# Order of the phases in one period of a two-layer graph attention kernel: score products, mask multiplications and GpSimd's sums on a Trainium2 core

## Chip, core and metric

The kernel runs on one core of a Trainium2 chip. The metric is the device time of one launch in microseconds (us), lower is better. Engines are named as the profile names them: PE is TensorE (matmuls, with PEld for its weight loads), DVE is VectorE, ACT is ScalarE, POOL is GpSimd, SP is SyncE (which issues nearly all DMAs).

## What is computed

64 graphs of 256 nodes with 512 features pass through two attention layers. Layer 0 has 8 heads of 64 features, layer 1 has 4; everything is float32. Shortened:

```python
h = relu(layernorm(x))                      # layer 0
m = h @ map_w.T + map_b
n = m_heads / norm(m_heads)
cos = n @ n.T ; cos_adj = (cos * ~adj) > 0.1
q, k = m @ q_w.T, m @ k_w.T
p = softmax(where(adj, -1e10, q k.T / 8)) * keep
A = cos_adj * p
x = x + relu((A @ (h @ gcn_map_w.T)) @ gcn_W.T / (A.sum(-1) + 1))
h = relu(layernorm(x))                      # layer 1
q, k, v = h @ Wq, h @ Wk, h @ Wv
attn = softmax(where(adj, q k.T / 8, -max))
x = x + (attn @ v) @ Wo + bo
```

## The kernel before

All instructions of all engines are issued in an order written out by hand (`manual_schedule`): each engine executes its own instructions in the order in which the code emits them, and semaphores between engines are put in where one instruction needs another's result or its buffer. The unit of the order is `period(i)` (line 556). A period works on up to four graphs at once: layer 0's attention of graph `g` (number i), layer 1's attention of graph `b` (i-1), the projections of layer 0 for `nx` (i+1), and the normalised, transposed input of `n2` (i+2). There are 65 periods, of which most have all four.

Projections are done by a seven-product scheme on halves (`seven_products`, line 260). It is a generator: each `next(...)` emits one portion. For the map (`m`), messages (`s`), queries (`q`), keys (`k`) and layer 1's queries and keys (`j`), the order of the `next` calls decides the order of the matmuls. A product group's result tile "z" (`pz`, line 311) is used several times in a row: the next portion writes it as soon as DVE has read the previous contents with `out(...)` (line 301).

Attention of a graph goes by head pairs: `NKC` = 4 pairs for layer 0, `NIC` = 2 for layer 1. For each pair c:
- `products` (line 395) forms transposed scores. Each matmul contracts over 64 rows only, so two heads run side by side in two halves of the array. Such matmuls read "64*128" in the profile, the projections "128*128".
- `exps` (line 404) takes the exponentials on ACT, from two PSUM banks into the SBUF tile `e` (128 x 1024 in all).
- `masked` (line 411) multiplies by the mask on DVE: one instruction of 128 x 1024 (line 417 for layer 0, line 415 for layer 1).
- `halves` (line 419) adds the two halves of `e` along the nodes on POOL into `d` (line 421): the first part of the softmax's denominator.
- Layer 0 only: `units` (line 382) multiplies the map by reciprocal lengths on DVE (one instruction of 128 x 1024, line 384), `cosines` (line 431) forms the cosine products from it, again with 64 rows, and `far_off` (line 442) thresholds them: ACT makes a small tile `up`, and DVE overwrites `e` in four instructions (line 451). `far_added` and `far_back` (lines 456 and 460) correct `d` on POOL by what was left (lines 458 and 465), and `far_back` finishes `e` on DVE (line 463). As `far_off` overwrites `e`, it has to come after `halves` of the same pair has read it.

`halved` (line 351) calls `left_factors` (line 250): four POOL instructions on the finished map `mT` (lines 254 to 257, tile `sm`). `shifts` (line 220) is a short DVE chain for `n2`: a reciprocal (line 201) and an instruction of 128 x 2 (line 224) that reads two SBUF operands.

PSUM is one ring of eight banks: each new tile takes the bank of the tile eight allocations earlier and waits until that one has been read.

Of the kernel before, what the change touches and what calls it, by code (L numbers as in the profile page):

```python
# [147 lines left out]
def fast_path(ctx, tc, a, w, chk, out):  # L148
# [8 lines left out]
    H0, NKC = D // DH, D // P  # L157
    INNER = a["Wq"].shape[1]
    H1, NIC = INNER // DH, INNER // P
# [81 lines left out]
    def join(g, k):  # L241
        nc.scalar.copy(g.bits[:, k], g.turn[:, k])
# [108 lines left out]
    def halved(g):  # L351
        g.left_m = left_factors(g.mT, "sm", g.i)
# [29 lines left out]
    def units(g):  # L382

        nc.vector.tensor_mul(g.nT, g.nT, g.mT)
# [10 lines left out]
    def products(rows, cols, c, name):  # L395

        ps = [bank(f"{name}_{s}", [P, NT, S]) for s in range(2)]
        for j in range(NT):
            for s in range(2):
                h = slice(s * DH, (s + 1) * DH)  # L400
                nc.tensor.matmul(ps[s][:, j, :], rows[h, c, j * P:(j + 1) * P], cols[h, c, :], start=True, stop=True)  # L401
        return ps

    def exps(ps, name):

        e = sb2.tile([P, 2, NT * S], F32, tag="e", name=f"e{name}", bufs=6)
        for s, p in enumerate(ps):
            nc.scalar.activation(e[:, s, :], p.rearrange("p j q -> p (j q)"), AF.Exp, scale=SCALE)  # L408
        return e

    def masked(e, mask, edges):

        m = mask.rearrange("p j q -> p (j q)")[:, None, :].to_broadcast([P, 2, NT * S])
        if edges:
            nc.vector.scalar_tensor_tensor(e, m, 0.5, e, op0=ALU.is_lt, op1=ALU.mult)  # L415
        else:
            nc.vector.tensor_mul(e, e, m)  # L417

    def halves(e, name):
        d = sb2.tile([P, 2, S], F32, tag="d", name=f"d{name}", bufs=6)  # L420
        nc.gpsimd.tensor_add(d, e[:, :, :S], e[:, :, S:])  # L421
        return d
# [133 lines left out]
    def period(i):  # L556
        g = graphs.get(i) if i < B else None
        b, nx, n2 = graphs.get(i - 1), graphs.get(i + 1), graphs.get(i + 2)
        def off_edges(cs):
            for c in cs if g else ():  # L560
                masked(g.e[c], g.mask, edges=False)
                g.d[c] = halves(g.e[c], f"0_{i}_{c}")


        if b:
            b.e1 = [exps(products(b.k1T, b.q1T, c, f"sc1_{b.i}_{c}"), f"1_{b.i}_{c}") for c in range(NIC)]
            for c in range(NIC):
                masked(b.e1[c], b.mask, edges=True)
            if b.last:
                for t in range(NT):  # L570
                    values_in(b, t)
            else:
                b.d1 = [halves(b.e1[c], f"1_{b.i}_{c}") for c in range(NIC)]
        if nx:
            m, s = mapped(nx), messages(nx)
            next(m)
        if g:
            for c in range(NKC):
                g.e[c] = exps(products(g.kT, g.qT, c, f"sc0_{i}_{c}"), f"0_{i}_{c}")
        if nx:  # L580
            next(s)
        off_edges((0, 1))
        if nx:
            next(m)
        off_edges((2,))
        if nx:
            next(m)
            next(s)
            next(m)
            halved(nx)  # L590

        if g:
            for c in range(NKC):
                far_off(g, c, cosines(g, c))
                if c == 0:
                    off_edges((3,))
            for c in range(NKC):
                far_added(g, c)
        if n2:
            shifts(n2, f"0_{n2.i}")  # L600
        if nx:
            q = queries(nx)
            next(q)
            next(s)
        if n2:
            sent(n2, f"0_{n2.i}", 0)
        if nx:
            next(q)
            squares(nx)
            next(s)  # L610
        if n2:
            sent(n2, f"0_{n2.i}", 1)
        for c in range(NKC):
            if g:
                far_back(g, c)
            if nx and c < 3:
                next((q, s, q)[c])
        if nx:
            lengths(nx, norms(nx))

        if i == 0:
            w.finish_seven(w.wqk1)
        if b:
            sums1(b)
            values1(b)
        if g:
            g.avs = sb1.tile([P, NKC, S], F32, tag="wide", name=f"avs{i}")
            g.sms = sb1.tile([P, S], F32, tag="sms", name=f"sms{i}")
            values(g, 0)
            values(g, 1)  # L630
            sums(g)
        if n2:
            joined(n2, f"0_{n2.i}")
            join(n2, 0)
        if nx:
            k = keys(nx)
            next(k)
        if b:
            nc.scalar.activation(b.rz, b.rz, AF.Copy, accum_out=chk[:, b.i, 3:4])
        if g:  # L640
            sums_back(g)
            heads_back(g)
        if n2:
            join(n2, 1)
        if nx:
            next(k)
        if n2:
            edges(n2)
        if b:
            divided(b)  # L650
        if g:
            moments(g, f"1_{i}")
        if nx:
            next(k)
        if g:
            deviations(g)
        if g:
            normalized(g, f"1_{i}")
        if nx:
            nc.scalar.activation(nx.rn, nx.rn, AF.Sqrt)  # L660

        nc.scalar.activation(spare[:, 1:], spare[:, :1], AF.Exp)
        if b:
            for t in range(NT):
                result(b, t)
                if b.last:
                    nc.sync.dma_start(out=out_t[b.i][:, t], in_=b.xs[:, t])
            if not b.last:
                nc.sync.dma_start(out=out_t[b.i], in_=b.xs)
        if i + 3 < B:  # L670
            graphs[i + 3] = load(i + 3)
        if g:
            g.h1T = turned(g, f"1_{i}", "wide")
            j = queries_keys1(g)
            for t in range(NT):
                nc.gpsimd.tensor_add(g.xs[:, t, :], g.xs[:, t, :], w.bo_b)
        if nx:
            next(k)
        if g:
            next(j)  # L680
        if nx:
            nc.vector.reciprocal(nx.rn, nx.rn)
            spread(nx)
        if g:
            next(j)
        if g:
            next(j)
            if not g.last:
                values_in(g, 0)
            next(j)  # L690
        if n2:
            n2.left_h = left_factors(n2.hT, "sh", n2.i)
        if i + 3 < B:
            moments(graphs[i + 3], f"0_{i + 3}")
        if g and not g.last:
            values_in(g, 1)
        if nx:
            units(nx)

    def normal_input(g):  # L700
        g.hT = turned(g, f"0_{g.i}", "hT")
# [2 lines left out]
    with tc.manual_schedule():  # L704
        spare = small.tile([P, 2], F32, tag="spare", name="spare", bufs=1)
        nc.vector.memset(spare, 0.0)
        graphs = {0: load(0)}
        w.load_map()
        gws = [sb2.tile([P, 2, D], F32, tag="e", name=f"gw{k}", bufs=6) for k in range(2)]
        w.load_folded(gws)  # L710
        w.load_scores()
        graphs.update({n: load(n) for n in range(1, min(3, B))})
        w.load_rest()

        def normal(n):
            moments(graphs[n], f"0_{n}")
            deviations(graphs[n])
            normalized(graphs[n], f"0_{n}")

        g = graphs[0]  # L720
        normal(0)
        normal_input(g)
        edges(g)
        w.finish_seven(w.wm)
        m = mapped(g)
        next(m)
        next(m)
        w.fold(gws, bank, w.put_seven)
        next(m)
        w.finish_seven(w.wq)  # L730
        next(m)
        halved(g)
        squares(g)
        w.finish_seven(w.wk)
        q, k, s = queries(g), keys(g), messages(g)
        next(q)
        lengths(g, norms(g))
        w.fold_bias(sb2.tile([P, NKC, P], F32, tag="xn", name="gbb"), bank)
        w.finish_seven(w.wc)
        for step in (k, q, k, q, k, q, k):  # L740
            next(step)
        nc.scalar.activation(g.rn, g.rn, AF.Sqrt)
        nc.vector.reciprocal(g.rn, g.rn)
        spread(g)
        if B > 1:
            edges(graphs[1])
            normal(1)
        nc.scalar.activation(spare[:, 1:], spare[:, :1], AF.Exp)
        for _ in range(5):
            next(s)  # L750
        units(g)
        if B > 1:
            normal_input(graphs[1])
        if B > 2:
            moments(graphs[2], "0_2")
        for i in range(B + 1):
            period(i)
# [298 lines left out]
```

## Time and profile before

| | |
|---|---|
| median of 3 runs | 3695.11 us (3693.84 to 3696.11) |
| span of the profiled execution | 3695.8 us, TensorE clock granted 0.996 |
| PE busy | 3651.0 us (99%) |
| PE weight loads | 3091.7 us (84%) |
| DVE busy | 2774.1 us (75%) |
| ACT busy | 1904.1 us (52%) |
| POOL busy | 2348.0 us (64%) |

The steady periods are equal: the score products of successive graphs start 56.58 us apart. A timeline lists the instructions of an engine in order of time, successive ones of the same kind merged: start (us from the span's start), duration, engine, line, operation, output <- inputs, shapes, count, and in brackets the idle time before it and what ended it. All times named below are of the period whose first score product starts at 1813.46 us; later periods repeat it 56.58 us further on. In fp32 each matmul and weight load of the code is two records.

### The profile page before, as it was taken

The page shows a single profiled execution, that of the slowest core. Times are in us where ns is not written, and L with a number is a line of the kernel's source. Part 1 is how long each engine was busy: PE and PEld are TensorE (multiplying, and loading weights), DVE is VectorE, ACT ScalarE, POOL GpSimd, SP SyncE. Part 2 cuts the span into 40 slices and gives each one's busy share as a digit, 9 for nine tenths or more (in the row PEclk, how much of TensorE's full clock was granted, in tenths as well). Part 3 has the DMA queues.
Part 4 walks back from the last instruction along what each step waited for, and adds up shares of the span by engine and source line. Part 5 has one row for each costly group of instructions (what it writes and reads, how often), then busy time and mean ns, then how long its engine had stood idle before and what let it go on. Part 6 is the DMA issues. An engine that isn't in the chain of part 4 may idle for free.

```text
span 3695.8 us, 76415 instructions
## 1 busy us (share of the span) xinstructions
PE 3651.0 (99%) x29153; PEld 3091.7 (84%) x29153; DVE 2774.1 (75%) x5288; ACT 1904.1 (52%) x4480; POOL 2348.0 (64%) x2044
## 2 busy tenths in 40 slices
PE   7999999999999999999999999999999999999997
PEld 7888888888888888888888888888888888888885
DVE  6777777777777777777877777777777777777775
ACT  3555555555555555555555555555555555555543
POOL 3667566666665665666766666666666667566663
PEclk9999999999999999999999999999999999999998
DMA  3111211211211112112112121121121112211211
GB/s 109 46 50 50 57 44 54 60 42 53 56 47 54 45 53 59 43 53 59 43 54 51 50 57 44 53 60 43 52 56 46 54 47 52 58 43 53 60 29 35
DMA packets 361008, 191.71 MB, mean 52 GB/s; under 512 B 272449, under 2 KB 326977, under 8 KB 360641
## 3 DMA queue, kind: packets, MB, share of 16 engines
q1 hardware_dynamic: 358368, 186.76, 19.0%
q8 instruction: 232, 3.80, 0.4%
q14 instruction: 136, 1.11, 0.1%
q10 hardware_dynamic: 2272, 0.04, 0.0%
HBM read 94.67 MB, written 34.34 MB: 35 GB/s over the span
## 4 chain that ended last, share of the span: by engine, by line
PE 96%; DVE 1%; DMA 1%; POOL 0%; issue 0%; ACT 0%; SPq 0%; DVEq 0%; ACTq 0%; POOLq 0%
PE sc L401 9%; PE av L428 9%; PE p_k L276 6%; PE p_q L276 6%; PE p_m L276 6%; PE p_qk L276 6%; PE p_s L271 6%; PE p_o L553 6%; PE p_v L520 6%; PE p_q_z L276 5%; PE co L438 5%; PE p_qk_z L276 5%; PE p_k_z L276 5%; PE p_m_z L276 5%; PE p_s_z L271 4%; PE sm L481 2%
## 5 line engine op out<-in xcount | busy, mean ns | idle before, releaser
L421 POOL TENSOR_TENSOR d<-e 128x512 f32<-128x512 f32 x382 | 716.2, 1900 | 199.5 <-DVE e L415 191.6
L408 ACT ACTIVATE e<-sc 128x512 f32<-128x512 f32 x768 | 389.9, 620 | 382.1 <-PE sc L401 375.6
L417 DVE TENSOR_TENSOR e<-e,mask 128x1024 f32<-128x1024 f32 x256 | 465.0, 1836 | 55.0 <-ACT e L408 55.0
L506 POOL TENSOR_TENSOR xs<-xs,o 128x512 f32<-128x512 f32 x128 | 188.5, 1494 | 385.5 <-DVE o L504 385.5
L465 POOL TENSOR_TENSOR d<-d,e 128x512 f32<-128x512 f32 x252 | 321.3, 1275 | 170.9 <-DVE e L463 169.2
L254 POOL TENSOR_TENSOR sh<-hT 128x256 f32<-128x256 f32 x128 | 93.6, 731 | 495.1 <-ACT hT L217 317.8
L458 POOL TENSOR_TENSOR d<-d,e 128x512 f32<-128x512 f32 x252 | 312.2, 1268 | 0.0
L451 DVE SCALAR_TENSOR_TENSOR e<-co,e 128x256 f32<-128x256 f32 (+1 forms) x1024 | 282.0, 343 | 35.8 <-ACT up L448 34.7
L448 ACT ACTIVATE up<-co,below 128x128 bf16<-128x128 f32 x512 | 159.6, 366 | 183.2 <-PE co L438 177.4
L553 PE MATMUL p_o<-wo,own 128*128 128x512 f32 x512 | 234.0, 600 | 9.8 <-DVE own L548 9.8
L520 PE MATMUL p_v<-wv,hT 128*128 128x256 f32 x1024 | 242.2, 379 | 0.0
L401 PE MATMUL sc<-qT,kT 64*128 64x256 f32 x2048 | 238.3, 382 | 0.0
L428 PE MATMUL av<-e,sem 128*64 128x256 f32 x2048 | 232.7, 380 | 0.0
L463 DVE SCALAR_TENSOR_TENSOR e<-far,e 128x256 f32<-128x256 bf16 x256 | 230.9, 903 | 0.0
L401 PEld LDWEIGHTS sc<-qT,kT 64*128 64x128 f32 x2048 | 192.9, 187 | 27.5
L428 PEld LDWEIGHTS av<-e,sem 128*64 128x64 f32 x2048 | 147.1, 137 | 75.2 <-DVE e L463 1.1
L491 DVE RECIPROCAL r<-rt 128x16 f32<-128x16 f32 x64 | 16.5, 258 | 253.3 <-PE rt L489 253.3
L520 PEld LDWEIGHTS p_v<-wv,hT 128*128 128x128 f32 x1024 | 184.9, 190 | 20.2 <-issue 0.3
L194 DVE BATCH_NORM_STATS2 st<-xs 128x6 f32<-128x512 f32 x256 | 173.8, 679 | 25.1 <-POOL xs L506 22.1
L438 PE MATMUL co<-nT 64*128 64x256 f32 (+1 forms) x2048 | 184.9, 330 | 0.0
L553 PEld LDWEIGHTS p_o<-wo,own 128*128 128x128 f32 x512 | 93.6, 193 | 104.7 <-issue 101.7
L231 ACT ACTIVATE xn<-xs,shift,rs 128x512 f32<-128x512 f32 x124 | 100.5, 810 | 156.1 <-POOL d L458 153.6
(198 smaller groups left out, 9350.0 us busy)
## 6 DMA issues: line engine op xcount, KB each, us to landing
xs<-in_x_dram SPq DMA_DIRECT2D x64, 512.0 KB
nT<-by_rn SPq DMA_DIRECT2D x128, 256.0 KB
out_dram<-xs SPq DMA_DIRECT2D x63, 512.0 KB
own<-by_rz SPq DMA_DIRECT2D x128, 128.0 KB
ad<-in_adj_dram SPq DMA_DIRECT2D x64, 64.0 KB
far<-up SPq DMA_TRANSPOSE x256
turn<-flat SPq DMA_TRANSPOSE x248
mask<-adb SPq DMA_TRANSPOSE x128
```

The lines of the kernel that those rows point to most:

```text
L271: nc.tensor.matmul(region, src[:, c, :], wt[:, block, c, :], start=p not in opened, stop=True, skip_group_check=True)
L276: nc.tensor.matmul(region[:, f, :], wt[:, block, c, f * P:(f + 1) * P], src[:, c, :], start=p not in opened, stop=True, skip_group_check=True)
L401: nc.tensor.matmul(ps[s][:, j, :], rows[h, c, j * P:(j + 1) * P], cols[h, c, :], start=True, stop=True)
L408: nc.scalar.activation(e[:, s, :], p.rearrange("p j q -> p (j q)"), AF.Exp, scale=SCALE)
L417: nc.vector.tensor_mul(e, e, m)
L421: nc.gpsimd.tensor_add(d, e[:, :, :S], e[:, :, S:])
L428: nc.tensor.matmul(av[s * DH:(s + 1) * DH, n, :], vs[:, j, (h0 + s) * DH:(h0 + s + 1) * DH], q[:, s, j * S:(j + 1) * S], start=(j == 0), s ...
L438: nc.tensor.matmul(ps[s][:, j, j * P:], g.nT[h, c, j * P:(j + 1) * P], g.nT[h, c, j * P:], start=(j == 0), stop=True, skip_group_check=True)
L458: nc.gpsimd.tensor_add(g.d[c], g.d[c], g.e[c][:, :, :S])
L465: nc.gpsimd.tensor_add(g.d[c], g.d[c], g.e[c][:, :, S:])
L520: nc.tensor.matmul(g.p_v[:, t, :], g.h1T[:, c, t * P:(t + 1) * P], w.wv1[:, c, :], start=(c == 0), stop=(c == NKC - 1))
L553: nc.tensor.matmul(p, b.avs1[:, c, t * P:(t + 1) * P], w.wo1[:, c, :], start=(c == 0), stop=(c == NIC - 1))
```

## The change

Within `period`:

1. Layer 0's score products and exponentials (four pairs) are emitted right behind layer 1's (two pairs). Before, the map's first portion stood between them. The map's and messages' first portions follow both.
2. Mask multiplication and `halves` are separated. POOL's `halves` of pairs 1 and 0 are emitted after the second mask of layer 0, pair 1 first; those of layer 1 (`b.d1`) come after them, where before they were first.
3. `units` of graph g moves from the end of the previous period to behind the first two masks.
4. The third mask (pair 2) moves from between the map's portions to behind the map's last portion and `halved(nx)`. Its `halves` moves to behind the fourth mask, together with pair 3's.
5. In the loop of `far_back`, the `next` call now comes ahead of `far_back` of the same turn.

```diff
-        def off_edges(cs):
+        def off_edges(*cs):
             for c in cs if g else ():
                 masked(g.e[c], g.mask, edges=False)
+
+        def halved_sums(*cs):
+            for c in cs if g else ():
                 g.d[c] = halves(g.e[c], f"0_{i}_{c}")
         if b:
             b.e1 = [exps(products(...)) for c in range(NIC)]
+        if g:
+            for c in range(NKC):
+                g.e[c] = exps(products(g.kT, g.qT, c, ...), ...)
+        if b:
             for c in range(NIC):
                 masked(b.e1[c], b.mask, edges=True)
             ...
-            else:
-                b.d1 = [halves(b.e1[c], f"1_{b.i}_{c}") for c in range(NIC)]
         if nx:
             m, s = mapped(nx), messages(nx)
             next(m)
-        if g:
-            for c in range(NKC):
-                g.e[c] = exps(products(g.kT, g.qT, c, ...), ...)
-        if nx:
             next(s)
-        off_edges((0, 1))
+
+        off_edges(0, 1)
+        halved_sums(1, 0)
+        if b and not b.last:
+            b.d1 = [halves(b.e1[c], f"1_{b.i}_{c}") for c in range(NIC)]
+        if g:
+            units(g)
         if nx:
             next(m)
-        off_edges((2,))
-        if nx:
             next(m)
             next(s)
             next(m)
             halved(nx)
+        off_edges(2)
 
         if g:
             for c in range(NKC):
                 far_off(g, c, cosines(g, c))
                 if c == 0:
-                    off_edges((3,))
+                    off_edges(3)
+                    halved_sums(2, 3)
             for c in range(NKC):
                 far_added(g, c)
 ...
         for c in range(NKC):
+            if nx and c < 3:
+                next((q, s, q)[c])
             if g:
                 far_back(g, c)
-            if nx and c < 3:
-                next((q, s, q)[c])
 ...
         if g and not g.last:
             values_in(g, 1)
-        if nx:
-            units(nx)
 ...                                          # start-up, ahead of the first period
         for _ in range(5):
             next(s)
-        units(g)
```

## The prediction

> **What bounds the kernel now.** I read the page first, then one steady period by stretches, then PE's timeline, then DVE and POOL beside it.
>
> ```profile
> PE 3651.0 (99%) x29153; PEld 3091.7 (84%) x29153; DVE 2774.1 (75%) x5288; ACT 1904.1 (52%) x4480; POOL 2348.0 (64%) x2044
> ...
> PE 96%; DVE 1%; DMA 1%; POOL 0%; issue 0%; ACT 0%; SPq 0%; DVEq 0%; ACTq 0%; POOLq 0%
> ```
> ```profile
> 1813.46:1870.04 56.58, 56.58 (x456) 47.99 (x455) 43.02 (x83) 29.82 (x70) 36.92 (x34) 1.00 0.19 51
> ```
>
> The first line is busy time by engine, the second the chain that ended last; the third is one period: length, then busy PE, PEld, DVE, ACT, POOL. PE has work through all 56.58 us. So only two things move the time: PE needing less time for the same matmuls, or PE starting to wait. PE's timeline of the touched stretch:
>
> ```profile
> 1813.46 2.00 PE L401 MATMUL sc<-qk 64*128 64x256 f32 x16
> 1815.39 2.05 PE L276 MATMUL p_m<-hT,wm 128*128 128x128 f32 x16
> 1817.37 3.72 PE L401 MATMUL sc<-qT,kT 64*128 64x256 f32 x32
> 1821.02 1.13 PE L271 MATMUL p_s<-wc,hT 128*128 128x256 f32 x4
> 1821.99 1.05 PE L276 MATMUL p_m_z<-hT,wm 128*128 128x128 f32 x8
> 1822.88 1.95 PE L276 MATMUL p_m<-sh,wm 128*128 128x128 f32 x16
> 1824.67 1.06 PE L276 MATMUL p_m_z<-sh,wm 128*128 128x128 f32 x8
> ```
>
> From start to start, 16 map matmuls between two score blocks take 1.98 us, the 16 among their own kind (1822.88) 1.79. Going between 64 and 128 rows costs time. DVE and POOL in the stretch that follows:
>
> ```profile
> 1828.84 1.15 DVE L451 SCALAR_TENSOR_TENSOR e<-co,e 128x256 f32<-128x256 f32 x4 [0.56 <-ACT up L448]
> 1829.90 1.74 DVE L417 TENSOR_TENSOR e<-e,mask 128x1024 f32<-128x1024 f32 x1
> 1831.57 3.25 DVE L451 SCALAR_TENSOR_TENSOR e<-co,e 128x256 f32<-128x256 f32 x12
> 1834.75 0.15 DVE L201 RECIPROCAL rs<-rs 128x2 f32<-128x2 f32 x1
> 1834.93 1.01 DVE L224 SCALAR_TENSOR_TENSOR shift<-mv,rs 128x2 f32<-128x2 f32 x1
> 1835.86 0.41 DVE L301 TENSOR_TENSOR sem<-p_s_z,u2p_s 128x256 f32<-128x256 f32 x1
> ```
> ```profile
> 1829.84 0.72 POOL L256 TENSOR_TENSOR sm<-mT 128x256 f32<-128x256 f32 x1
> 1830.53 1.70 POOL L257 TENSOR_TENSOR sm<-mT,sm 128x256 f32<-128x256 f32 x1
> 1832.20 1.27 POOL L421 TENSOR_TENSOR d<-e 128x512 f32<-128x512 f32 x1
> 1833.43 4.96 POOL L458 TENSOR_TENSOR d<-d,e 128x512 f32<-128x512 f32 x4
> ```
>
> The mask (1829.90) and POOL's `sm` obstruct each other: a mask takes 1.21 us at its fastest, 1.74 here; `sm` 0.72, or 1.70. `sem` at 1835.86 ends at 1836.27 and frees the tile that PE's next `p_s_z` overwrites at 1837.39. That is 1.1 us of slack.
>
> **What the Trainium skill says.** "SBUF — State Buffer", section "SBUF: two separate sides": one port pair of VectorE and GpSimd is an exclusive lock, taken for a whole instruction by whoever starts first, by GpSimd or by a DVE instruction with two SBUF inputs. The trace agrees: `sm` started at 1829.84, the mask 0.06 us later; the mask ran only after it, and the next `sm` after the mask (1831.6 + 0.7 = its end at 1832.23). I read L224's 1.01 us for 256 elements likewise: it starts 0.27 us behind an L458 instruction (these start every 1.23 us, so 1834.66) and ends with it. DVE instructions with a PSUM operand don't slow down beside POOL. "TensorEngine Tiling (Array Packing)", "Key Properties": changing the tiling mode drains TensorE; that is the 1.98 against 1.79.
>
> **The change part by part**, against the profiled span of 3695.8 us (0.7 above the median, within the three runs).
>
> *Scores in one phase.* Now `sc` 1.93, `p_m` 1.98, `sc` 3.65, first `p_s` 0.97: 8.53 us from 1813.46 to 1821.99. Sixteen more score matmuls without a switch cost 3.65 - 1.93 = 1.72, so 48 take 5.37; `p_m` loses the switch behind it (1.88), `p_s` the one ahead (0.87, as at 1825.56). Sum 8.12: PE is **0.41 us earlier** per period. No bank stops this: 12 score tiles on 8 banks need ACT to have emptied the first four when PE reaches the ninth, about 1817.0; ACT's first exponential starts at 1814.68 and they follow each 0.5, so these four end by 1816.75.
>
> *First masks, units, sums held.* With POOL's sums held, masks 0 and 1 take 1.13 each from start to start, now 3.58 for two. `units` (1.21) follows, about 1820.4 to 1821.6. Cosines need it at 1827.0: hidden. POOL's four sums then run from about 1821.5 to 1826.5, before `mT` is whole: hidden; `zb` and the totals read them 15 us later.
>
> *Third mask, its sum, and what is queued behind.* `mT` is whole at 1827.87 (now 1828.27, less 0.41). Mask 2 then starts about 1827.8 and, 0.15 ahead of POOL's first `sm`, takes the lock to 1829.0. `far_off` of pair 0 follows at 1828.93 (four instructions, 1.06), and frees the bank that PE's `p_q` wants at 1829.8 by 1829.55: just no wait. POOL: `sm` from 1828.87, two by 1830.38; mask 3, at DVE since 1829.99, gets the lock then and ends at 1831.46; the other two `sm` end at 1832.73. Only then come the sums of pairs 2 and 3: 1.27 each, ending 1833.97 and 1835.19. This is a **new wait**: in the changed program's instruction order, `far_off` of pairs 2 and 3 waits for these two POOL sums, which read `e` before it is overwritten. (Before, pair 2's sum was done before `sm` began, pair 3's at 1833.47.) DVE, free at 1832.45, waits 1.6 us, does pair 2, waits again to 1835.23 for pair 3, reaches L201 at 1836.3 and L224 at 1836.47 to 1836.52. POOL starts L458's second instruction at 1835.16 + 1.23 = 1836.39, so L224 loses the lock by about 0.1 us and ends with it, 1837.67. `sem` ends at 1838.0, and PE's `p_s_z` starts at 1838.07. It wanted to at 1836.98; before it did at 1837.39: **0.68 us later** than before, the 0.41 included. Queued behind on DVE: `u5p_s`, `qT`, then ACT's `xn` for the next input, whose `u5p_q` now ends about 1840.25; the following `p_q_z` then starts near 1840.8, against 1840.06. A restart without prefetched weights adds up to 0.1. I take +0.7 per period; bounds +0.45 (restart free, PE's present 0.1 us wait there gone) and +1.0.
>
> *far_back behind the evacuations.* Same instructions, other order; `e` of pair 3 is finished about 0.3 us later, and PE reads it last of four, 2 us on: nothing. SP's transposes of `turn` start 1.7 us later; PE's delay and ACT's later copy (1848.99) hide that.
>
> *Edges.* Periods 1 to 61: 61 x 0.7 = 42.7. Period 0 has no layer 1, so no switch is saved but the wait is there: +1.1. Period 62 has no `shift` and gains 0.4. In period 63 no projections cover DVE, and `units` lies on its path: +2 (bounds 0 and 3). Sum **+45: span 3741, median 3740 us**.
>
> **Rivals.**
> (1) *L224 gets the lock.* Were DVE 0.1 to 0.15 us earlier at L224, or POOL later, it would cost 0.15 instead of 1.2 us; `sem` would end at 1837.0, just when PE wants its tile. Then the saved switches remain: -0.35 x 61, -0.4 in period 62, +2 at the end, 3695.1 - 19.8: about 3675. For it: the margin is a tenth of a microsecond, from rows of other instructions. Against: today POOL wins with 0.06 against a mask. This is the side opposite to my forecast.
> (2) *Partial cancelling.* Locks change hands quicker than read, the new wait takes just what the switches gave, or both orders occur: -0.1 to +0.1 per period, 3690 to 3703.
> (3) *More than one new wait.* `p_q` misses its bank, or ACT's later `xn` and squares hold up `p_n` too: +1.0 to +1.4, 3760 to 3785.
> That the change doesn't do what it says is excluded by the built order: scores are adjacent, sums stand where described.
>
> **Chances and range.** Forecast 0.62 (its own range 3725 to 3758, from the bounds per period), rival 1 0.21, rival 2 0.07, rival 3 0.10. This kernel's measurement tells about 0.2%, 7 us, from no change. Slower: forecast and rival 3, 0.72; same 0.06; faster 0.22. For 8 in 10 the range must reach into rival 1: 3674 to 3758.
>
> **What would show it.** Right: scores merged without a gap, `p_m` about 5.35 us behind the first score; PE idle around 1 us before the second `p_s_z`, put down to DVE; DVE's L451 waiting for POOL's sums, some 1.6 us per period; L224 still near 1.2; a period near 57.3. Masks 0 and 1 at 1.21 each would confirm the hold. Wrong: a period of 56.2 with L224 at 0.15 is rival 1; L451 without a wait for POOL means that the new wait is my invention.

## The result, and the profile after

| | before | changed |
|---|---|---|
| median of 4 runs each | 3694.48 us (3692.95 to 3696.11) | 3740.96 us (3738.94 to 3741.73) |
| ratio, 95% interval | | 1.0125 [1.0107, 1.0142] |
| span of the profiled execution | 3695.8 us | 3737.2 us |
| steady period (median, first score product to the next) | 56.58 us | 57.31 us |
| last full interval, between the last two graphs' scores | 42.75 us | 44.11 us |

The kernel became slower by 46 us. The forecast was 3740 us. The 61 steady periods account for it: summed, they take 3452.2 us before and 3496.3 after, 44.1 more. (The two profiled spans differ by only 41.4: the first layer-1 score of the changed profile comes at 111.97 us, that of before at 115.66. Over all the profiles here this start-up lies between 109.7 and 115.7 us, with no order by kernel, so periods are the surer measure.)

The page of the changed kernel, its busy times, the chain that ended last, and two groups (busy, mean ns of one | idle time ahead of them and what ended it):

```profile
PE 3634.9 (97%) x29153; PEld 3092.7 (83%) x29153; DVE 2626.2 (70%) x5288; ACT 1898.0 (51%) x4480; POOL 2224.4 (60%) x2044
...
PE 79%; DVE 11%; POOL 6%; issue 3%; DMA 1%; ACT 0%; SPq 0%; ACTq 0%; DVEq 0%; POOLq 0%
...
L417 DVE TENSOR_TENSOR e<-e,mask 128x1024 f32<-128x1024 f32 x256 | 325.2, 1291 | 1.7 <-ACT e L408 1.7
...
L451 DVE SCALAR_TENSOR_TENSOR e<-co,e 128x256 f32<-128x256 f32 (+1 forms) x1024 | 293.4, 348 | 100.2 <-POOL d L421 95.1
```

The same two groups before:

```profile
L417 DVE TENSOR_TENSOR e<-e,mask 128x1024 f32<-128x1024 f32 x256 | 465.0, 1836 | 55.0 <-ACT e L408 55.0
L451 DVE SCALAR_TENSOR_TENSOR e<-co,e 128x256 f32<-128x256 f32 (+1 forms) x1024 | 282.0, 343 | 35.8 <-ACT up L448 34.7
```

PE was 99% busy and is 97% busy; DVE and POOL, which now stand in the chain with 17%, are *less* busy than before, by 148 and 124 us. So neither ran out of throughput. A mask now takes 1291 ns on average (1836 before). What is new is in the last field of L451: DVE idles 95.1 us, waiting for POOL's sums, where before it idled 34.7 us for ACT's `up`.

The same period by stretches (length; busy PE, PEld, DVE, ACT, POOL), its PE timeline, then DVE's and POOL's. Its clock is the prediction's plus 18.01 us.

```profile
1831.47:1888.78 57.31, 56.40 (x457) 48.09 (x456) 40.73 (x83) 29.71 (x70) 34.91 (x34) 1.00 0.18 51
```
```profile
1831.47 2.00 PE L401 MATMUL sc<-qk 64*128 64x256 f32 x16
1833.30 3.62 PE L401 MATMUL sc<-qT,kT 64*128 64x256 f32 x32
1836.85 2.05 PE L276 MATMUL p_m<-hT,wm 128*128 128x128 f32 x16
1838.74 1.03 PE L271 MATMUL p_s<-wc,hT 128*128 128x256 f32 x4
1839.60 1.05 PE L276 MATMUL p_m_z<-hT,wm 128*128 128x128 f32 x8
...
1853.21 1.95 PE L276 MATMUL p_q<-sm,wq 128*128 128x128 f32 x16
1856.07 1.13 PE L271 MATMUL p_s_z<-wc,sh 128*128 128x256 f32 x4 [0.91 <-DVE sem L301]
```
```profile
1836.09 2.35 DVE L417 TENSOR_TENSOR e<-e,mask 128x1024 f32<-128x1024 f32 x2
...
1845.80 1.21 DVE L417 TENSOR_TENSOR e<-e,mask 128x1024 f32<-128x1024 f32 x1
1846.94 1.14 DVE L451 SCALAR_TENSOR_TENSOR e<-co,e 128x256 f32<-128x256 f32 x4
1848.00 1.49 DVE L417 TENSOR_TENSOR e<-e,mask 128x1024 f32<-128x1024 f32 x1
1849.41 1.14 DVE L451 SCALAR_TENSOR_TENSOR e<-co,e 128x256 f32<-128x256 f32 x4
1852.02 2.38 DVE L451 SCALAR_TENSOR_TENSOR e<-co,e 128x256 f32<-128x256 f32 x8 [1.47 <-POOL d L421]
1854.31 0.16 DVE L201 RECIPROCAL rs<-rs 128x2 f32<-128x2 f32 x1
1854.50 1.18 DVE L224 SCALAR_TENSOR_TENSOR shift<-mv,rs 128x2 f32<-128x2 f32 x1
1855.61 0.41 DVE L301 TENSOR_TENSOR sem<-p_s_z,u2p_s 128x256 f32<-128x256 f32 x1
```
```profile
1845.96 1.64 POOL L254 TENSOR_TENSOR sm<-mT 128x256 f32<-128x256 f32 x1 [1.57 <-DVE mT L301]
1847.68 0.73 POOL L255 TENSOR_TENSOR sm<-sm,mT 128x256 f32<-128x256 f32 x1
1848.36 1.71 POOL L256 TENSOR_TENSOR sm<-mT 128x256 f32<-128x256 f32 x1
1850.04 0.72 POOL L257 TENSOR_TENSOR sm<-mT,sm 128x256 f32<-128x256 f32 x1
1850.72 2.49 POOL L421 TENSOR_TENSOR d<-e 128x512 f32<-128x512 f32 x2
1853.17 4.96 POOL L458 TENSOR_TENSOR d<-d,e 128x512 f32<-128x512 f32 x4
```

Read from the end. PE could have gone on at 1855.00, since 16 of the `p_q` matmuls take 1.79 us from the first start to the next instruction's start where nothing waits; it started `p_s_z` at 1856.07. (The bracket says 0.91, because it counts from the recorded end of the last `p_q`, which overlaps what follows.) PE waited for `sem`, which ended at 1856.02 (1855.61 + 0.41) and stood behind L224, 1.18 us for 256 elements. L224 stood behind L451, which could go on with pair 2 only at 1852.02, when POOL's first sum had ended (1851.98), and with pair 3 only when the second had (1853.21). And the sums stood behind four `sm`, two of them 1.64 and 1.71 us long, because each mask held the lock ahead of one.

### The profile page after: what moved, and what is told of

Its sections match the earlier page's. It is cut to its first block, busy times and chain, and to the rows that moved or that the text cites. A ratio compares the mean times of both kernels' runs of the same rounds, so it can differ in the third digit from the quotient of the medians.

```text
span 3737.2 us, 76479 instructions
## 1 busy us (share of the span) xinstructions
PE 3634.9 (97%) x29153; PEld 3092.7 (83%) x29153; DVE 2626.2 (70%) x5288; ACT 1898.0 (51%) x4480; POOL 2224.4 (60%) x2044
## 4 chain that ended last, share of the span: by engine, by line
PE 79%; DVE 11%; POOL 6%; issue 3%; DMA 1%; ACT 0%; SPq 0%; ACTq 0%; DVEq 0%; POOLq 0%
PE sc L401 9%; PE av L428 9%; PE p_k L276 6%; PE p_m L276 6%; PE p_qk L276 6%; PE p_o L553 6%; PE p_v L520 6%; DVE e L451 5%; PE p_qk_z L276 5%; PE p_k_z L276 5%; PE p_m_z L276 5%; POOL d L421 4%; PE p_s_z L271 3%; DVE e L417 3%; PE p_q_z L276 3%
## 5 line engine op out<-in xcount | busy, mean ns | idle before, releaser
L421 POOL TENSOR_TENSOR d<-e 128x512 f32<-128x512 f32 x382 | 534.4, 1426 | 365.0 <-DVE e L417 365.0
L451 DVE SCALAR_TENSOR_TENSOR e<-co,e 128x256 f32<-128x256 f32 (+1 forms) x1024 | 293.4, 348 | 100.2 <-POOL d L421 95.1
L417 DVE TENSOR_TENSOR e<-e,mask 128x1024 f32<-128x1024 f32 x256 | 325.2, 1291 | 1.7 <-ACT e L408 1.7
L458 POOL TENSOR_TENSOR d<-d,e 128x512 f32<-128x512 f32 x252 | 312.1, 1269 | 0.0
L271 PE MATMUL p_s_z<-wc,sh 128*128 128x256 f32 x512 | 139.4, 395 | 59.7 <-DVE sem L301 59.2
L463 DVE SCALAR_TENSOR_TENSOR e<-far,e 128x256 f32<-128x256 bf16 x256 | 190.1, 762 | 0.0
```

Of the source, the lines that this page charges most:

```text
L271: nc.tensor.matmul(region, src[:, c, :], wt[:, block, c, :], start=p not in opened, stop=True, skip_group_check=True)
L451: nc.vector.scalar_tensor_tensor(e, p.rearrange("p j q -> p (j q)")[:, lo:hi], THRESHOLD, e, op0=ALU.is_gt, op1=ALU.mult)
L458: nc.gpsimd.tensor_add(g.d[c], g.d[c], g.e[c][:, :, :S])
```

## The experiments

Theory: the loss is this chain, and it comes from part 4 alone. Steady periods below are medians over the profiled execution; each median is of 4 runs (5 for a6), and the ratio is to runs of the kernel before on the same chip.

| | edit | median us | ratio, 95% interval | period us |
|---|---|---|---|---|
| changed kernel | | 3740.96 | 1.0125 [1.0107, 1.0142] | 57.31 |
| a1_third_back | part 4 undone | 3663.77 | 0.9913 [0.9897, 0.9930] | 56.08 |
| a2_sums_first | `sm` behind the sums | 3666.91 | 0.9920 [0.9904, 0.9937] | 56.08 |
| a3_shift_later | L224 behind the evacuations | 3741.71 | 1.0125 [1.0108, 1.0142] | 57.32 |
| b1_scores_only | before, with part 1 | 3668.47 | 0.9925 [0.9908, 0.9941] | 56.18 |
| a4_one_sum_first | one sum ahead of `sm` | 3758.48 | 1.0169 [1.0152, 1.0186] | 57.59 |
| b4_third_only | before, with part 4 | 3767.56 | 1.0197 [1.0180, 1.0214] | 57.76 |
| a6_act_order | as a3, `xn` later too | 3680.71 | 0.9961 [0.9947, 0.9975] | 56.36 |
| b15_scores_far_back | before, with parts 1 and 5 | 3662.38 | 0.9910 [0.9894, 0.9927] | 56.08 |
| a6b_shift_last | as a6, L224 later still | 3867.08 | 1.0473 [1.0456, 1.0491] | 58.72 |
| a5_far_back_first | part 5 undone | 3744.32 | 1.0139 [1.0122, 1.0156] | 57.37 |
| a6c_sqrt_first | as a6b, ACT's root early | 3665.07 | 0.9918 [0.9901, 0.9934] | 56.08 |

### Is it part 4, and in it the place of the sums?

a1: the changed kernel with the third mask back between the map's portions, its sum ahead of `sm`.

```diff
             units(g)
         if nx:
             next(m)
+        off_edges(2)
+        halved_sums(2)
+        if nx:
             next(m)
             next(s)
             next(m)
             halved(nx)
-        off_edges(2)
...
                     off_edges(3)
-                    halved_sums(2, 3)
+                    halved_sums(3)
```

> The changed kernel with the third mask back between the map's portions and pair 2's sum ahead of the four sm instructions; scores merged, first sums held, units and far_back as changed. Theory (POOL's sums of pairs 2 and 3 queued behind sm hold up DVE, whose L224 then waits once more for the lock, until PE waits at the second p_s_z): pair 2's sum is done before sm, pair 3's about 2 us earlier than in the changed kernel, PE waits nowhere, and the saved switches remain: period 56.1 to 56.2, about 3668. Rival (the loss lies in other parts of the change, the held first sums or units in the period): still near 57.3 per period, about 3740.

a2: everything stays in its new place, the third mask too, but `halved(nx)` is emitted behind the two sums.

```diff
             next(m)
-            halved(nx)
         off_edges(2)
...
                     halved_sums(2, 3)
+                    if nx:
+                        halved(nx)
             for c in range(NKC):
                 far_added(g, c)
+        elif nx:
+            halved(nx)
```

> The changed kernel with one edit: the four sm instructions are emitted behind POOL's sums of pairs 2 and 3; the third mask stays where the change put it. Theory: pair 3's sum ends about 1832.8 on the prediction's clock in place of 1835.2, DVE passes L224 before PE wants the tile, sm is whole about 0.5 us before p_q needs its last part: period 56.1 to 56.2, about 3668. Rival (it is the place of the third mask that costs, its 1.2 us on DVE between the map and far_off, not POOL's queue): no gain, about 3740.

Both give a period of 56.075 us, 1.23 less than the changed kernel, with PE busy throughout: DVE's and POOL's timelines of a2 show why.

```profile
1810.69 1.22 DVE L417 TENSOR_TENSOR e<-e,mask 128x1024 f32<-128x1024 f32 x1
1811.82 1.15 DVE L451 SCALAR_TENSOR_TENSOR e<-co,e 128x256 f32<-128x256 f32 x4
1812.88 1.52 DVE L417 TENSOR_TENSOR e<-e,mask 128x1024 f32<-128x1024 f32 x1
1814.32 3.25 DVE L451 SCALAR_TENSOR_TENSOR e<-co,e 128x256 f32<-128x256 f32 x12
```
```profile
1812.05 1.27 POOL L421 TENSOR_TENSOR d<-e 128x512 f32<-128x512 f32 x1 [2.78 <-DVE e L417]
1814.54 1.27 POOL L421 TENSOR_TENSOR d<-e 128x512 f32<-128x512 f32 x1 [1.23 <-DVE e L417]
```

Mask 2 stands where the change put it, and yet L451 runs twelve in a row without a wait, since each sum follows its mask at once. So the third mask's place is not the cause; that its sum is queued behind `sm` is. L224 is short here (0.33 us), but that alone isn't what brings the gain: in a1 it takes 1.18 us again, but begins 21.50 us into the period against 23.04 in the changed kernel, and PE doesn't wait. L224's length decides only when DVE is already late.

b4 asks the same from the other side: part 4 alone, on the kernel before.

```diff
-        off_edges((2,))
...
             halved(nx)
+        if g:
+            masked(g.e[2], g.mask, edges=False)
...
-                    off_edges((3,))
+                    masked(g.e[3], g.mask, edges=False)
+                    for h in (2, 3):
+                        g.d[h] = halves(g.e[h], f"0_{i}_{h}")
```

> The kernel before with part 4 alone: third mask behind the map's portions and the sm instructions, sums of pairs 2 and 3 behind the fourth mask; scores as before. Theory: the whole chain from the finished map to p_s_z is as in the changed kernel, without the saved switches and with far_back's old order: period 57.3 + 0.40 = 57.7, or up to 57.9; 3763 to 3775. Rival (the loss needs the merged scores or the held first sums as well): 3700 or less.

57.76 against 56.58: part 4 costs 1.18 us per period by itself, as against 1.23 within the changed kernel. Its DVE timeline has the same row of L451 with the same wait, 1.47 us for `d`, and L224 at 1.18. The cause is part 4, and it needs none of the other parts.

### What are the others worth?

b1: the kernel before with part 1 alone (the score products of layer 0 moved up, nothing else).

```diff
             b.e1 = [exps(products(...)) for c in range(NIC)]
+        if g:
+            for c in range(NKC):
+                g.e[c] = exps(products(g.kT, g.qT, c, ...), ...)
...
-        if g:
-            for c in range(NKC):
-                g.e[c] = exps(products(g.kT, g.qT, c, ...), ...)
```

> The kernel before with part 1 alone: layer 0's scores right behind layer 1's, all else as before. Theory: two switches fewer save 0.41 us in 61 periods: about -25 us, 3669. Rival (the merged scores alone cost something, a bank of the ring or a mask that comes later): 3690 or more.

56.183 against 56.579: 0.396 us per period, where the prediction had 0.41. Two changes of the tiling mode are saved, so one costs about 0.2 us.

b15: part 5 added to it.

```diff
         for c in range(NKC):
-            if g:
-                far_back(g, c)
             if nx and c < 3:
                 next((q, s, q)[c])
+            if g:
+                far_back(g, c)
```

> The kernel before with parts 1 and 5: merged scores, and the far_back loop with next first. Theory (held first sums and units in the period bring nothing, since DVE has time there; part 5 saves 0.1 us of PE's wait at p_q_z): period 56.08 as in the run with the third mask put back, and 3661 to 3664, since units stay out of the last period. Rival (held sums or units brought the 0.1 us): period 56.18, 3668.

56.075: another 0.108 us. The portions that `next` emits end with evacuations, the DVE instructions that read a product's PSUM tile and so free it for PE. In b1 `far_back` of pair 0 stands ahead of one of them on DVE, `uup_q` (L321), for which PE's last `p_q_z` waits. In b15 `uup_q` starts 0.11 us earlier, that `p_q_z` 0.05 earlier, and everything on PE from `p_n` on 0.11 earlier; up to there PE's instructions start equally. This kernel has the shortest median of all, 3662.38 us, though a1 and a6c lie within 3 us of it.

That sorts out parts 2 and 3. a1 has parts 1, 2, 3 and 5; b15 has 1 and 5; their periods are equal. Holding POOL's sums and moving `units` is worth nothing per period, though a mask takes 1508 ns on average in a1 and 2061 in b15. In the last interval the two parts together cost time: 44.11 us in a1 as in the changed kernel, 40.96 in b15.

a5: the changed kernel with part 5 undone.

```diff
         for c in range(NKC):
-            if nx and c < 3:
-                next((q, s, q)[c])
             if g:
                 far_back(g, c)
+            if nx and c < 3:
+                next((q, s, q)[c])
```

> The changed kernel with part 5 undone (far_back ahead of next, as before). Without the new wait part 5 was worth 0.11 us per period. Theory (uup_q waits 0.18 us for ACT's u5p_q in the changed kernel, and far_back of pair 0, 0.33 us, would come in that gap and 0.15 beyond): period 57.4 to 57.5, 3744 to 3752. Rival (with PE late at p_s_z, part 5 is worth nothing): 57.31, 3741.

57.37 against 57.31: 0.06 us, about half of the 0.11 that part 5 brings where PE doesn't wait. The median is within the theory's range, the period just under it, and the traces show the theory's reason: in the changed kernel `uup_q` waits 0.18 us for ACT's `u5p_q` anyway. With part 5 undone `far_back` of pair 0 fills that wait, and `uup_q` starts only 0.07 us later.

With this run parts 2 and 3 can be told beside part 4 as well. b4 with part 1's gain taken off makes 57.758 - 0.396 = 57.362; a5, which has parts 1 to 4, measured 57.370. So they add nothing there either.

### Which link of the chain costs PE the time?

a3: `shifts(n2)` (L201, L224) moved behind the evacuations that PE waits for.

```diff
-        if n2:
-            shifts(n2, f"0_{n2.i}")
         if nx:
             q = queries(nx)
             next(q)
             next(s)
         if n2:
+            shifts(n2, f"0_{n2.i}")
+        if n2:
             sent(n2, f"0_{n2.i}", 0)
```

> The changed kernel with one edit: the shifts (L200, L201, L224) are emitted behind the p_q and p_s portions that they stood ahead of, so that DVE frees p_s_z first; POOL's queue is untouched and far_off of pairs 2 and 3 waits as before. Theory (both links are needed: the late POOL sums and L224's wait for the lock): sem ends about 1.3 us earlier, just when PE wants the tile; period 56.1 to 56.4, 3670 to 3685. Rival (the wait for POOL's sums alone is enough): p_s_z still waits 0.5 us or more, period 56.8 or more, 3710 or more.

A miss: the period stayed at 57.32. The PE timeline, then DVE and ACT:

```profile
1855.85 1.03 PE L271 MATMUL p_s_z<-wc,sh 128*128 128x256 f32 x4
...
1859.65 1.16 PE L276 MATMUL p_q_z<-sm,wq 128*128 128x128 f32 x8 [0.69 <-DVE uup_q L321]
```
```profile
1859.17 0.42 DVE L321 TENSOR_TENSOR uup_q<-p_q_z,u5p_q 128x256 f32<-128x256 f32 x1 [1.37 <-ACT u5p_q L293]
```
```profile
1856.63 0.81 ACT L231 ACTIVATE xn<-xs,shift,rs 128x512 f32<-128x512 f32 x1 [3.20 <-POOL d L458]
1857.47 1.14 ACT L234 COPY flat<-xn 128x512 uint16<-128x512 uint16 x2
1858.52 0.62 ACT L293 ACTIVATE u5p_q<-p_q,bq 128x128 f32<-128x128 f32 x2
```

`p_s_z` no longer waits; the last `p_q_z` does. For `xn` needs `shift`, and it stands on ACT ahead of `u5p_q`, which DVE's `uup_q` needs, and that frees the tile of the next `p_q_z`. (The releaser that the trace infers for `xn`, a sum of POOL that ACT doesn't read, is a wrong guess; by the code it is DVE's `shift`, which ends at 1856.55, 0.08 ahead of it.) So `shift` is ready 24.2 us into the period, as in the changed kernel: L224 lost less at the lock, but came later. The delay had two ways to PE, one beside the other; closing the first left the second, which is as long.

a6 closes both: `shifts` as in a3, and `sent(n2, 0)`, with `xn` and `flat`, behind the next queries and squares.

```diff
-        if n2:
-            shifts(n2, f"0_{n2.i}")
...
         if n2:
-            sent(n2, f"0_{n2.i}", 0)
+            shifts(n2, f"0_{n2.i}")
         if nx:
             next(q)
             squares(nx)
+        if n2:
+            sent(n2, f"0_{n2.i}", 0)
+        if nx:
             next(s)
```

> The changed kernel with shifts behind the first portions, as in the run that moved shifts alone, and with ACT's xn for the next input (sent, first half) behind u5p_q and the squares. POOL's queue and DVE's wait for it stay. Theory (two waits in series behind DVE's delay: L224 ahead of sem, then ACT's xn ahead of u5p_q): with both out of the way PE waits nowhere, though DVE still waits 1.5 us for POOL: period 56.1 to 56.2, 3664 to 3672. Rival (DVE's wait for POOL costs PE time by some other way, a bank or far_back): 3690 or more.

56.36, and 3680.71 us: between the theory's range and the rival's. 0.96 of a3's 1.25 us above 56.075 is gone. What is left, 0.29, comes with a wait of PE's weight load for `qT` (28.9 us in 62 times by the waits), which stands behind L224's 0.52 us on DVE. a6b was to remove that too, with `shifts` behind the second `next(q)` and the squares (the edit is shown against a3).

```diff
             next(s)
+            next(q)
+            squares(nx)
         if n2:
             shifts(n2, f"0_{n2.i}")
             sent(n2, f"0_{n2.i}", 0)
         if nx:
-            next(q)
-            squares(nx)
             next(s)
```

> As the run that moved shifts and ACT's xn, but with shifts (and the first half of sent behind it) behind the second p_q portion and the squares, so that L224 no longer stands ahead of qT on DVE either. POOL's queue and DVE's wait of 1.47 us for it stay. Theory (the wait for POOL costs PE only through what is queued behind it on DVE and, in turn, on ACT; the 0.29 us per period left in that run are L224's wait ahead of qT): period 55.95 to 56.1, 3657 to 3666. Rival (the rest comes from DVE being late as such): still 56.3 or more, 3677 or more.

58.72, a miss, by an edit that moved more than was meant. `shifts` begins with ACT's square root (L200), and that moved too:

```profile
1862.08 0.17 DVE L201 RECIPROCAL rs<-rs 128x2 f32<-128x2 f32 x1 [3.07 <-ACT rs L200]
1862.28 0.16 DVE L224 SCALAR_TENSOR_TENSOR shift<-mv,rs 128x2 f32<-128x2 f32 x1
```

L224 takes 0.16 us, and DVE waits 3.07 us for the root ahead of it, with `uup_s` queued behind. a6c leaves the root where it was and moves only DVE's two instructions, with `sent` behind them (the edit is shown against the changed kernel).

```diff
-        deviations(g)
+        nc.vector.reciprocal(g.rs, g.rs)
...
         if n2:
-            shifts(n2, f"0_{n2.i}")
+            nc.scalar.activation(n2.rs, n2.rs, AF.Sqrt)
...
             next(s)
+            next(q)
+            squares(nx)
         if n2:
+            shifts(n2, f"0_{n2.i}")
             sent(n2, f"0_{n2.i}", 0)
         if nx:
-            next(q)
-            squares(nx)
             next(s)
```

> The run before it, a6b_shift_last, moved ACT's square root with its table load behind the squares as well, so that DVE's L201 stood 3.07 us waiting for ACT ahead of uup_s: a wait of its own making. Here the square root keeps its early place on ACT; only DVE's L201 and L224 and ACT's xn stand behind qT and the squares. POOL's queue and DVE's wait of 1.47 us for it stay. Theory (DVE's wait for POOL costs PE only through what is queued behind it): period 55.95 to 56.1, 3657 to 3666. Rival (DVE being late costs as such): 56.3 or more, 3677 or more.

```profile
1816.68 2.38 DVE L451 SCALAR_TENSOR_TENSOR e<-co,e 128x256 f32<-128x256 f32 x8 [1.47 <-POOL d L421]
1818.97 0.41 DVE L301 TENSOR_TENSOR sem<-p_s_z,u2p_s 128x256 f32<-128x256 f32 x1
...
1820.15 0.20 DVE L224 SCALAR_TENSOR_TENSOR shift<-mv,rs 128x2 f32<-128x2 f32 x1
```

56.075 us, all of the loss gone, and DVE still waits the same 1.47 us for POOL. The wait of DVE as such costs PE nothing: what costs is the sum of the wait and of what is queued between it and the instructions that release PE.

### Half of the remedy

a4: only pair 2's sum ahead of `sm`.

```diff
             next(m)
-            halved(nx)
         off_edges(2)
+        halved_sums(2)
+        if nx:
+            halved(nx)
...
-                    halved_sums(2, 3)
+                    halved_sums(3)
```

> The changed kernel with pair 2's sum alone moved ahead of the four sm instructions on POOL (behind the third mask, which stays); pair 3's stays behind them. The visible wait of DVE, 1.47 us ahead of far_off of pair 2, should vanish. Theory (pair 3's sum, last in POOL's queue, sets when DVE gets on): the same POOL work stands ahead of it, so the wait moves to pair 3 and PE waits as before: period 57.2 to 57.4, 3735 to 3745. Rival (the 1.47 us wait that the trace shows is what is lost): period near 56.1, 3668.

57.59, more than the changed kernel. The theory's range, 57.2 to 57.4, was missed, and the rival's 56.1 by far more. DVE, then POOL:

```profile
1857.12 1.22 DVE L417 TENSOR_TENSOR e<-e,mask 128x1024 f32<-128x1024 f32 x1
...
1860.75 2.19 DVE L451 SCALAR_TENSOR_TENSOR e<-co,e 128x256 f32<-128x256 f32 x8
1864.86 1.15 DVE L451 SCALAR_TENSOR_TENSOR e<-co,e 128x256 f32<-128x256 f32 x4 [1.91 <-POOL d L421]
```
```profile
1858.48 1.27 POOL L421 TENSOR_TENSOR d<-e 128x512 f32<-128x512 f32 x1 [2.77 <-DVE e L417]
1859.71 1.71 POOL L254 TENSOR_TENSOR sm<-mT 128x256 f32<-128x256 f32 x1
...
1863.56 1.26 POOL L421 TENSOR_TENSOR d<-e 128x512 f32<-128x512 f32 x1
```

The wait moved from pair 2 to pair 3, as the theory had it: POOL has the same six instructions to do, and pair 3's sum is still last. From the start of mask 2 to the end of that sum are 7.70 us here (1857.12 to 1864.82), 7.41 in the changed kernel (1845.80 to 1853.21). The difference, 0.29, is that of the periods, 0.28. I put it to how POOL starts: in the changed kernel `sm` is already at the lock and ends as if it had begun at 1846.88 (1847.60 less 0.72), 0.13 before the mask's recorded end at 1847.01; the sum here needs the mask's result and starts 0.14 after the end. That is read from two timelines; no run isolates it.

## Why the prediction was right

The forecast was 3740 us; measured were 3740.96. By its own steps:

- *Scores in one phase.* Predicted 8.12 us from the first score to `p_m_z`, measured 8.13. `p_m` came 5.38 behind the first score (5.37). b1 gives the part's worth alone, 0.396 against 0.41. The step's evidence that no bank stops the scores holds too: no gap stands between them.
- *First masks.* 1.13 each from start to start was forecast, 1.14 measured (the timeline's 2.35 us runs to the end of the second). Right, and as said it hides: b15, without the hold, has the longer masks and a1's period.
- *Third mask, `sm`, sums.* Every station is within 0.03 us, once the clock is shifted by 18.01: second `sm` ended at 1848.41 (predicted 1848.39), mask 3 at 1849.49 (1849.47), the last `sm` at 1850.76 (1850.74), the second sum at 1853.21 (1853.20).
- *The new wait.* Predicted 1.6 us for the first sum and a short one for the second. The first is 1.47; the second is within the eight L451 that the timeline merges, 2.38 us long where eight without a wait in a4 took 2.19. L201 came at 1854.31, as predicted (1836.3, to a tenth).
- *L224 loses the lock.* The step with the smallest margin, 0.1 us, on which rival 1 hung. L224 started at 1854.50, L458's second instruction at about 1854.40 (1853.17 + 1.23), and L224 ended 0.02 us after that one did. Its minimum over 62 is 1170 ns: it lost every time. Rival 1 falls.
- *What is queued behind.* `p_s_z` came at 1856.07, 1.08 us later than in a1, where it does not wait (1.09 predicted). The last `p_q_z` started at 1858.80; predicted was near 1858.8. The way through `xn` and `u5p_q` was named as well, as something that follows; a3 shows that it is a bound of its own, of the same size.
- *Per period.* +0.73 against +0.7. The sum was -0.41 + 1.09 = 0.68 and something for the restart; measured are -0.396 (part 1), -0.108 (part 5) and +1.23. Laid beside a1 (medians of 30 periods), `p_s_z` starts 1.08 later in the period; the `p_q_z` after it 1.18, which is the restart's 0.10 that was named as an upper bound; and `p_n` and all after it 1.23.
- *`far_back`, "nothing".* This term was mis-sized: it is worth 0.11 us per period where PE has no other wait, and 0.06 here. The prediction's reason looked at who reads `e`, and not at what else comes sooner: the evacuations that go ahead of it. It had seen PE's 0.1 us wait, but only in the bounds. In the sum the gain nearly cancels with the restart and 0.05 more behind the last `p_q_z`, of which little was counted: that is luck.
- *Edges.* Period 62 takes 56.09 us against 56.60, a gain of 0.5 (0.4 predicted). The last interval lost 1.36 us (+2, bounds 0 and 3). Period 0 has the wait too, 0.92 us of idle time ahead of `p_s_z`, but the start-up varies too much to tell what it cost.

Rival 2 (the new wait takes just what the switches gave) needed a period of 56.5 to 56.7 and falls by 0.6; rival 3 needed +1.0 at least. That the sum fits to the microsecond is partly luck too: the start-up alone varies by 6 us over the profiles here.

## What to carry to other kernels

Before an instruction is moved behind others on a slow engine, ask who *overwrites* what it reads: the reader's delay becomes a wait of the writer, and then of everything queued behind the writer. Where the bound engine is released by an engine that has got a wait, list all queues behind that wait (here DVE's `sem`, ACT's `u5p_q`, DVE's `qT`); closing one changes nothing while another is as late. And judge a reordering that shortens instructions by the period, not by their durations: masks that were a quarter shorter were worth nothing here.

## What the runs showed of the hardware

In one run a wait of PE lowered the clock that it was granted. In a6b PE idled 2.30 us in each period ahead of `p_s_z`. Two successive periods by stretches, with one short stretch of the second; then the PE timeline of the second:

```profile
1776.36:1835.08 58.72, 56.42 (x456) 48.07 (x455) 39.69 (x83) 29.95 (x70) 34.94 (x34) 1.00 0.18 50
1835.08:1895.36 60.28, 57.98 (x456) 48.77 (x455) 39.67 (x83) 30.03 (x70) 34.91 (x34) 0.97 0.19 48
1864.17:1867.58 3.41, 3.41 (x26) 1.92 (x26) 3.41 (x8) 2.20 (x5) 2.45 (x2) 0.50 0.51 43
```
```profile
1862.83 1.13 PE L271 MATMUL p_s_z<-wc,sh 128*128 128x256 f32 x4 [2.30 <-DVE uup_s L321]
1863.82 1.77 PE L276 MATMUL p_q_z<-sm,wq 128*128 128x128 f32 x8
1865.52 1.08 PE L362 MATMUL p_n<-sq,blk 128*32 128x256 f32 x8
```

The granted clock (first figure behind the busy times) is 1.00 in the first period and 0.97 in the second; behind the gap, `p_q_z` takes 1.77 us and `p_n` 1.08, where without the loss they take 1.16 and 0.64. The loss is one stretch of 3.41 us at half the clock (the third line). 23 of the 61 steady periods have one such stretch each and are 1.6 us longer.

Which periods are hit can be worked out from the trace. The 23 stretches begin at whole multiples of 3.413 us from each other, to within 0.01, so they lie on one grid with cells of that length. Laid on this grid, the gap has 1.83 us or more of its 2.30 within one cell in each of the 23, and the next cell is the slow one; in the other 38 the gap is split so that no cell holds more than 1.80. So it was not the length of the gap alone that decided here, but its place on the grid. In the steady periods of the other kernels, whose longest gap is 1.48 us (in a4), no such stretch occurs. This is one run with one length of gap; no run tests the limit with others.

L224 shows what a small DVE instruction with two SBUF inputs can cost beside POOL. It takes 0.16 us in a6b, where no POOL instruction runs when it starts, and for the same 256 elements 0.20 in a6c, 0.33 in a2, 0.52 in a3 and a6, 1.01 in the kernel before and 1.18 in the changed one. In all of these it ends 0.01 to 0.03 us after the POOL instruction that was running when it started: its time is what that instruction had left.
